# Where a norm takes its reciprocal root: ScalarE's table and VectorE's reciprocal, or Newton's steps on GpSimd

## The chip, the cores and the metric

The kernel runs on one core of a Trainium2 chip, in one launch. A core has five engines that work side by side, each through its own instructions in order: PE (TensorE, matrix products into PSUM), DVE (VectorE), ACT (ScalarE), POOL (GpSimd) and SP (SyncE, which here only issues transfers). The metric is the device time of one execution in microseconds (us), the median of several; lower is better.

## The reference, cut to what matters

A block of six sublayers over 2048 positions of 256 features, all in float32: feed-forward, attention, feed-forward, then the same three with other weights. Each sublayer is preceded by a layer norm, and the feed-forward of the first kind has an RMS norm in its middle. These norms are what the change is about.

```python
def _layernorm(x, axis=-1, eps=1e-05):
    m = jnp.mean(x, axis=axis, keepdims=True)
    v = jnp.var(x, axis=axis, keepdims=True)
    return (x - m) / jnp.sqrt(v + eps)

def rms_norm(x):                       # inside _L0_ffn_ref, over 1024 hidden values
    eps = jnp.finfo(x.dtype).eps.astype(jnp.float32)
    xf = x.astype(jnp.float32)
    inv = jax.lax.rsqrt(jnp.mean(xf * xf, axis=-1, keepdims=True) + eps)
    return (xf * inv).astype(x.dtype)
...
x = x + 0.5 * _L0_ffn_ref(_layernorm(x, axis=-1), L0_ffn_w_gate_up, L0_ffn_w_proj)
x = x + _L0_attn_ref(_layernorm(x, axis=-1), L0_attn_W_qkv, L0_attn_W_o)
x = x + 0.5 * _L0_ffn_ref(_layernorm(x, axis=-1), L0_ffn_w_gate_up, L0_ffn_w_proj)
x = x + 0.5 * _L1_ffn_ref(_layernorm(x, axis=-1), L1_ffn_w_gate, L1_ffn_w_up, L1_ffn_w_down)
x = x + _L1_attn_ref(_layernorm(x, axis=-1), ...)
x = x + 0.5 * _L1_ffn_ref(_layernorm(x, axis=-1), L1_ffn_w_gate, L1_ffn_w_up, L1_ffn_w_down)
```

`_L0_ffn_ref` makes its weights ternary (per group of 64), takes `silu(gate) * up`, the RMS norm, and a projection. `_L1_ffn_ref` takes `silu(gate) * up`, keeps the two largest of every four hidden values, and projects. Both attentions are causal with 16 heads of 16.

## The kernel before

**Tiling.** Features lie on the 128 partitions (two halves of 128, `DC = 2`), positions along the free dimension, cut into four chunks of 512 (`CH`, `NCH`). A chunk of x stays in SBUF from start to end (`xs[c]`), its normed form in `xns[c]`. The stages are called f0, attention 0, f1, f2, attention 1, f3. In the times below they run about from 0 to 212, 212 to 755, 755 to 877, 877 to 1085, 1085 to 1645 and 1645 to 1830 us.

**A step.** The order of the work on PE, DVE, ACT and POOL is written out by the program itself, through Python generators that hand over at `yield`. In a feed-forward stage a step is one of the eight blocks of 128 hidden values of a chunk: `gate_up0` (L297) or `gate_up` (L271) multiplies on PE, `member` (L310) takes Silu on ACT (L313) and multiplies by `up` on DVE (L314). In stages f0 and f1, `parts_of` (L326) splits each block into a rounded part (ACT, L328) and a rest (DVE, L335), squares it (ACT, L333) and adds the squares on POOL (L334). In f2 and f3, `sparsify` (L398) compares and selects on DVE (L408 to L436). After a chunk's blocks the next chunk's steps carry its projection along: `tail0` (L349) or `tail1` (L441). At the start f0 also makes the weights ternary (`quantize`, L130), six DVE instructions for each of 12 tiles. In an attention a step is one block of 128 keys of one group of four heads: scores, maxima on DVE (L721), exponentials on ACT (L792), and products with the values on PE (L807).

**Background.** The layer norms of the chunks to come wait in a queue, `background`. Each step calls `pull` (L194), which moves the first two of them on to their next `yield`. `ready(c)` (L200) pulls until chunk c's norm is through. At the end of an attention `gate` holds norms back before their root.

**A layer norm** (L234) goes: sum of the two halves on POOL (L242); two or three steps later the mean by a matmul with the matrix `mean_m`, whose entries are 1/256 (L246); x minus mean on DVE (L248); squares on ACT (L251); their sum on POOL (L253); two steps later a matmul again (L259) and `root`; one step later `spread`, and two multiplies on POOL that write `xn` (L264).

**The RMS norm** in `tail0`: the sums of squares go through a matmul with `ones_m` (L373), then `root`, a step in between, the second half of the projection, `spread`, and then `add` (L365): a product on DVE (L367) and the addition to x on POOL (L368).

**`root` and `spread`** (L205 to L222). The matmul leaves every position's value in all 128 rows. DVE's transpose by blocks of 32 (L209) turns it so that a tile of 128 x 16 holds each value once per block; the root is taken on that small tile. ACT takes the square root with scale and eps (L211), DVE the reciprocal (L216), and a second transpose (L218) spreads the result over 128 x 512 again. ACT works its functions from a table that must be loaded; Sqrt, Silu and Exp lie in different ones, so that the compiler puts an ACT_TABLE_LOAD ahead of a root and another ahead of the next Silu or Exp. Abs, Sign, Square, copies and Identity need none.

**Queues.** SP issues nearly all transfers, ACT the four loads of x. No transfer is issued by POOL.

Of the kernel before, what the change touches and what calls it, by code (L numbers as in the profile page):

```python
# [12 lines left out]
F32 = mybir.dt.float32  # L13
BF16 = mybir.dt.bfloat16
F32R = mybir.dt.float32r
AF = mybir.ActivationFunctionType
ALU = mybir.AluOpType
AX = mybir.AxisListType
# [2 lines left out]
P = 128  # L21
S = 2048
E = 256
# [3 lines left out]
SLOT = 32  # L27
G = 4
F = 1024
FC = F // P  # L30
CH = 512
# [16 lines left out]
def macaron_kernel(ctx: ExitStack, tc: tile.TileContext, a, out):  # L48
    nc = tc.nc

    cpool = ctx.enter_context(tc.tile_pool(name="const", bufs=1))
# [10 lines left out]
    def ps_one(name):  # L62
        return ps3.tile([P, CH], F32, tag="one", name=name)
# [43 lines left out]

    mean_m = cpool.tile([P, P], F32, name="mean_m")
    nc.vector.memset(mean_m, 1.0 / E)
    ones_m = cpool.tile([P, P], F32, name="ones_m")  # L110
    nc.vector.memset(ones_m, 1.0)
    eps_ln = cpool.tile([P, 1], F32, name="eps_ln")
    nc.vector.memset(eps_ln, 1e-5)
    eps_rms = cpool.tile([P, 1], F32, name="eps_rms")
    nc.vector.memset(eps_rms, 4 * float(np.finfo(np.float32).eps))


    lpool = ctx.enter_context(tc.tile_pool(name="ln", bufs=1))
# [4 lines left out]
    w0pool = ffn0_scope.enter_context(tc.tile_pool(name="weights0", bufs=1, side="right"))  # L123
    wgu0 = w0pool.tile([P, DC, 2 * F], F32R, name="wgu0")
    wp0 = w0pool.tile([P, FC, E], F32R, name="wp0")
    raw_scope = ExitStack()
# [3 lines left out]
    def quantize(i):  # L130
# [19 lines left out]
        aw = qp.tile([P, 512], BF16, tag="aw", bufs=4, name=f"aw{i}")  # L150
        nc.scalar.activation(aw, raw, AF.Abs)
        sg = qp.tile([P, 512], BF16, tag="sg", bufs=4, name=f"sg{i}")
        nc.scalar.activation(sg, raw, AF.Sign)
        yield
# [50 lines left out]
    def root(ps, eps, scale, name):  # L205


        tt = lpool.tile([P, CH // SLOT, SLOT], F32, tag="tt", name=f"tt_{name}")
        nc.vector.transpose(tt.rearrange("p b s -> p (b s)"), ps)  # L209
        r = lpool.tile([P, CH // SLOT], F32, tag="r", bufs=3, name=f"r_{name}")  # L210
        nc.scalar.activation(r, tt[:, :, 0], AF.Sqrt, bias=eps, scale=scale)  # L211
        return r

    def spread(r, pool, bufs, name):

        nc.vector.reciprocal(r, r)  # L216
        sd = pool.tile([P, CH], F32, tag="sd", bufs=bufs, name=f"sd_{name}")
        nc.vector.transpose(  # L218
            sd.rearrange("p (b s) -> p b s", s=SLOT),
            r.unsqueeze(2).to_broadcast([P, CH // SLOT, SLOT]),  # L220
        )
        return sd  # L222


    def split(c, hp, name):

        xn = xns[c]
        top = hp.tile([P, DC, CH], F32R, tag="xtop", bufs=2, name=f"xt_{name}")
        nc.vector.tensor_copy(top, xn)
        rest = hp.tile([P, DC, CH], F32R, tag="xrest", bufs=2, name=f"xr_{name}")  # L230
        nc.vector.tensor_tensor(rest, xn, top.bitcast(F32), ALU.subtract)  # L231
        return top, rest

    def layernorm(c, name, slack=0):  # L234

        pending[c] += 1
        asked.add(name)

        def pieces():
            x, xn = xs[c], xns[c]  # L240
            s = lpool.tile([P, CH], F32, tag="s", bufs=2, name=f"s_{name}")
            nc.gpsimd.tensor_tensor(s, x[:, 0, :], x[:, 1, :], ALU.add)  # L242
            for _ in range(2 + slack):
                yield
            pm = ps_one(f"pm_{name}")
            nc.tensor.matmul(pm, lhsT=mean_m, rhs=s, start=True, stop=True)  # L246
            xc = lpool.tile([P, DC, CH], F32, tag="xc", bufs=2, name=f"xc_{name}")
            nc.vector.tensor_tensor(  # L248
                xc, x, pm.unsqueeze(1).to_broadcast([P, DC, CH]), ALU.subtract
            )  # L250
            nc.scalar.activation(xn, xc, AF.Square)  # L251
            v = lpool.tile([P, CH], F32, tag="s", bufs=2, name=f"v_{name}")
            nc.gpsimd.tensor_tensor(v, xn[:, 0, :], xn[:, 1, :], ALU.add)  # L253
            yield
            yield
            while gate[0]:
                yield
            pv = ps_one(f"pv_{name}")
            nc.tensor.matmul(pv, lhsT=mean_m, rhs=v, start=True, stop=True)  # L259
            r = root(pv, eps_ln, 1.0, f"ln_{name}")  # L260
            yield
            sd = spread(r, lpool, 2, f"ln_{name}")
            for dc in range(DC):
                nc.gpsimd.tensor_tensor(xn[:, dc, :], xc[:, dc, :], sd, ALU.mult)  # L264
            pending[c] -= 1
            yield

        return pieces()


# [39 lines left out]
    def member(pg, hp, name, to=None):  # L310
        sl = hp.tile([P, CH], F32, tag="sl", bufs=3, name=f"sl_{name}")
        to = sl if to is None else to
        nc.scalar.activation(sl, pg[:, 0, :], AF.Silu)  # L313
        nc.vector.tensor_tensor(to, sl, pg[:, 1, :], ALU.mult)  # L314
        return to

    def steps0(c, xp, hp, own, name):
# [3 lines left out]
        tops = [  # L321
            hp.tile([P, 4, CH], F32R, tag="hr", bufs=3, name=f"ht_{name}_{q}") for q in range(2)
        ]
        rests = hp.tile([P, FC, CH], F32R, tag="h", bufs=2, name=f"hl_{name}")

        def parts_of(f, h):  # L326
            top = tops[f // 4][:, f % 4, :]
            nc.scalar.copy(top, h)  # L328
            if f == 0:
                nc.scalar.activation(ss, h, AF.Square)  # L330
            else:
# [17 lines left out]
    def tail0(c, ss, parts, hp, own, name):  # L349


        def project(dc):
            po = ps_one(f"po_{name}_{dc}")
            for f in range(FC):
                for part in range(2):
                    nc.tensor.matmul(  # L356
                        po,
                        lhsT=wp0[:, f, dc * P : (dc + 1) * P],
                        rhs=parts[f][part],
                        start=f == 0 and part == 0,  # L360
                        stop=f == FC - 1 and part == 1,
                    )
            return po

        def add(dc, po):  # L365
            y = hp.tile([P, CH], F32, tag="sl", bufs=3, name=f"y_{name}_{dc}")
            nc.vector.tensor_tensor(y, po, inv, ALU.mult)  # L367
            nc.gpsimd.tensor_tensor(xs[c][:, dc, :], y, xs[c][:, dc, :], ALU.add)  # L368

        po = project(0)  # L370
        yield
        pss = ps_one(f"pss_{name}")
        nc.tensor.matmul(pss, lhsT=ones_m, rhs=ss, start=True, stop=True)  # L373
        r = root(pss, eps_rms, 4.0 / F, f"rms_{name}")
        yield
        after = project(1)
        inv = spread(r, own, 1, f"rms_{name}")
        add(0, po)
        yield
        add(1, after)  # L380
        yield
# [75 lines left out]
    def feed_forwards(stages, beside, own=None):  # L457


        with tc.tile_pool(name=f"ffn_{stages[0][1]}", bufs=1) as hp:  # L460
# [4 lines left out]
            for s, (kind, stage, order) in enumerate(stages):  # L465
                for at, c in enumerate(order):
# [32 lines left out]
                    if kind == 0:  # L499
                        try:  # L500
                            next(work)
                        except StopIteration as end:
                            tail = ((0, 1, 2, 3), tail0(c, *end.value, hp, own, name), done)
                    else:
                        last = s == len(stages) - 1 and c == order[-1]
                        tail = ((4, 5), tail1(c, h, name, last), done)
# [594 lines left out]

    load_x(0, nc.scalar)
    ln = layernorm(0, "f0_0")
    for k in range(6):
        next(ln)
        if k in (0, 2, 4, 5):
            next(quants[0])
            next(quants[0])
# [119 lines left out]
```

## Time and profile before

| what | us |
|---|---|
| median of 3 runs (lowest, highest) | 1829.09 (1828.29, 1836.65) |
| the profiled execution | 1831.77 |
| its span, first to last instruction | 1830.0 |
| PE busy | 1648.4 |
| DVE busy | 1314.3 |
| ACT busy | 911.8 |
| POOL busy | 347.0 |
| ACT_TABLE_LOAD for roots (L211), 24 | 30.8 |
| ACT_TABLE_LOAD for Silu (L313), 19 | 24.4 |
| ACT_TABLE_LOAD for Exp (L792), 8 | 10.3 |
| the roots themselves (L211), 32 | 10.3 |
| the reciprocals (L216), 32 | 7.5 |

By stage, the busy time of each engine and the share of its clock that PE was granted (the view by windows; after the times stand the numbers of instructions in brackets):

| window, us | PE | DVE | ACT | POOL | PE clock |
|---|---|---|---|---|---|
| 0 to 26 | 6.5 | 20.2 | 12.8 | 7.8 | 1.00 |
| 26 to 90 | 36.0 | 55.5 | 24.2 | 23.3 | 0.81 |
| 90 to 212 | 106.9 | 72.8 | 65.7 | 69.3 | 0.93 |
| 212 to 755 | 509.2 | 406.7 | 310.9 | 47.8 | 0.99 |
| 755 to 877 | 100.6 | 83.4 | 69.8 | 70.4 | 0.93 |
| 877 to 1085 | 198.0 | 138.4 | 64.8 | 45.6 | 0.98 |
| 1085 to 1645 | 518.6 | 425.7 | 316.8 | 71.1 | 0.98 |
| 1645 to 1700 | 48.0 | 38.6 | 21.2 | 11.8 | 1.00 |
| 1700 to 1830 | 124.6 | 73.1 | 25.6 | 0.0 | 1.00 |

How to read the lines that follow. A line of the timeline has the start from the span's start, the duration, the engine (a q behind it is its sequencer, which only issues or waits), the line of the program, the operation, out<-in by the program's names, the shape written<-read and the count; in square brackets stands how long the engine had been idle before it, and what ended that. A line of a group has xcount, then busy time and mean ns of one, then the idle time before them and its causes. A line of waits has who waited, for whom, and then us in total, times and the longest. PE's durations are modelled and overlap: of matmuls in a row, the starts tell the pace.

### The profile page before, as it was taken

The numbers are of one execution on the slowest core, as the hardware profiler recorded it, in microseconds if no ns is written. First come the engines' busy times: TensorE is split into PE (matmuls) and PEld (weight loads), VectorE is DVE, ScalarE is ACT, GpSimd is POOL, SyncE is SP. The second block draws the span as 40 slices with busy tenths as digits, with TensorE's granted clock in tenths as the row PEclk, the third lists the DMA queues.
The fourth block names the chain that finished last, engine by engine and source line by source line (L and its number), as shares of the span: only waits on it lengthen the run. The fifth ranks groups of instructions, "written<-read, shape, count | busy, mean of one in ns | idle before, by whom it ended". The sixth has DMA issues, their size and how long they took to land.

```text
span 1830.0 us, 26213 instructions
## 1 busy us (share of the span) xinstructions
PE 1648.4 (90%) x10299; PEld 782.5 (43%) x10300; DVE 1314.3 (72%) x2368; ACT 911.8 (50%) x1220; POOL 347.0 (19%) x346
## 2 busy tenths in 40 slices
PE   4498888999999999788899998899999999988999
PEld 2365543444434443366444444334434434433443
DVE  7865687787788884466666677778788888816664
ACT  4365354555565667555423325445565556674221
POOL 3355520200000001265411232122001000012000
PEclk9799899999999999999999999999999999999999
DMA  4003332212211110200000334222122110000000
GB/s 138 2 1 105 114 95 79 72 54 76 93 41 47 30 30 1 78 1 1 13 0 1 103 109 130 66 85 90 48 65 90 46 46 28 11 2 0 12 12 23
DMA packets 50508, 93.06 MB, mean 51 GB/s; under 512 B 5424, under 2 KB 33072, under 8 KB 50128
## 3 DMA queue, kind: packets, MB, share of 16 engines
q1 hardware_dynamic: 49296, 89.28, 15.9%
q10 hardware_dynamic: 1088, 2.10, 0.4%
q8 instruction: 81, 1.33, 0.3%
q14 instruction: 43, 0.35, 0.1%
HBM read 59.51 MB, written 27.26 MB: 47 GB/s over the span
## 4 chain that ended last, share of the span: by engine, by line
PE 62%; DVE 19%; ACT 4%; issue 2%; POOL 2%; DMA 1%; SPq 0%; DVEq 0%; ACTq 0%; POOLq 0%
PE pav L807 14%; PE pst L772 12%; PE pq L710 11%; DVE mx L721 8%; PE pg_f L276 7%; PE po_f L287 5%; PE pg_f L301 2%; PE pwo L848 2%; PE pp_k L557 2%; PE pp_q L557 1%; PE po_f L356 1%; DVE ge_f L408 1%; PE pv L622 1%; PE pst L780 1%; PE pq L718 1%
## 5 line engine op out<-in xcount | busy, mean ns | idle before, releaser
L721 DVE TENSOR_REDUCE mx<-pq 128x1 f32<-128x512 f32 (+3 forms) x1280 | 696.7, 602 | 132.8 <-PE pq L718 65.4
L792 ACT ACTIVATE pT<-pst 128x1024 f32<-128x1024 f32 (+3 forms) x616 | 536.2, 897 | 335.8 <-PE pst L772 170.7
L710 PE MATMUL pq<-k,q 105*128 105x512 bf16 (+7 forms) x1280 | 385.9, 349 | 53.2 <-DVE mx L721 46.4
L772 PE MATMUL pst<-q,k 99*128 99x512 bf16 (+7 forms) x1280 | 356.5, 352 | 10.6 <-ACT pT L792 6.7
L807 PE MATMUL pav<-pT,va 128*32 128x256 f32 (+1 forms) x4608 | 324.7, 377 | 6.2 <-DVE yt L828 5.0
L276 PE MATMUL pg_f<-xn,wgu 128*128 128x512 f32 x512 | 230.5, 602 | 15.0 <-DVE hr_f L314 15.0
L772 PEld LDWEIGHTS <-k 105*128 105x128 bf16 (+1 forms) x1280 | 111.5, 98 | 233.7 <-issue 168.3
L833 POOL TENSOR_TENSOR zt<-yt,rd 128x64 f32<-128x64 f32 x128 | 42.1, 329 | 807.3 <-DVE rd L832 803.0
L807 PEld LDWEIGHTS pav<-pT,va 128*32 128x32 f32 x4608 | 106.3, 108 | 191.5 <-issue 136.8
L710 PEld LDWEIGHTS <-q 105*128 105x128 bf16 (+1 forms) x1280 | 122.9, 98 | 128.9 <-issue 26.5
L313 ACT ACTIVATE sl_f<-pg_f 128x512 f32<-128x512 f32 x128 | 75.9, 593 | 174.7 <-PE pg_f L276 98.3
L276 PEld LDWEIGHTS pg_f<-xn,wgu 128*128 128x128 f32 x512 | 97.4, 192 | 142.8 <-issue 115.1
L301 PE MATMUL pg_f<-xt_f,wgu 128*128 128x512 f32 x256 | 101.0, 478 | 37.8 <-DVE sl_f L314 20.9
L287 PE MATMUL po_f<-h_f,wd 128*128 128x512 f32 x256 | 112.6, 593 | 1.4 <-DVE h_f L436 1.4
L718 PE MATMUL pq<-mask_qk,ident_b 128*128 128x128 bf16 x512 | 105.4, 222 | 0.0
L780 PE MATMUL pst<-mask_kq,ident_b 128*128 128x128 bf16 x512 | 103.1, 221 | 0.0
L334 POOL TENSOR_TENSOR ss_f<-ss_f,sq_f 128x512 f32<-128x512 f32 x56 | 85.2, 1521 | 88.8 <-ACT sq_f L333 88.2
L314 DVE TENSOR_TENSOR hr_f<-sl_f,pg_f 128x512 f32<-128x512 f32 x64 | 43.7, 683 | 69.1 <-ACT sl_f L313 68.8
L828 DVE STREAM_TRANSPOSE yt<-pav 128x128 f32<-128x128 f32 x128 | 39.8, 311 | 71.1 <-PE pav L807 71.1
L301 PE MATMUL pg_f<-xr_f,wgu 128*128 128x512 f32 x256 | 86.0, 419 | 1.5 <-DVE xr_f L231 1.5
L314 DVE TENSOR_TENSOR sl_f<-sl_f,pg_f 128x512 f32<-128x512 f32 x64 | 43.7, 682 | 60.2 <-ACT sl_f L313 59.8
L301 PEld LDWEIGHTS pg_f<-xt_f,wgu 128*128 128x128 f32 x256 | 51.7, 208 | 80.8 <-DVE sl_f L314 27.5
(134 smaller groups left out, 1755.1 us busy)
## 6 DMA issues: line engine op xcount, KB each, us to landing
k<-dk SPq DMA_DIRECT2D x80, 384.0 KB
dk<-p_k SPq DMA_DIRECT2D x48, 256.0 KB
dq<-p_q SPq DMA_DIRECT2D x48, 256.0 KB
q<-dq SPq DMA_DIRECT2D x32, 384.0 KB
x<-in_xT ACTq DMA_DIRECT2D x4, 512.0 KB
raw<-in_w_gu SPq DMA_DIRECT2D x8, 256.0 KB
wgu<-in_w_gu SPq DMA_DIRECT2D x1, 2048.0 KB
cs_k<-in_cos_sin SPq DMA_DIRECT2D x4, 512.0 KB
```

Source lines behind the costliest of these rows:

```text
L276: nc.tensor.matmul(pg[:, half, :], lhsT=wgu[:, dc, half * F + f * P : half * F + (f + 1) * P], rhs=xn[:, dc, :], start=dc == 0, stop=dc == ...
L287: nc.tensor.matmul(po, lhsT=w[:, f, dc * P : (dc + 1) * P], rhs=h[:, f, :], start=f == 0, stop=f == FC - 1,)
L301: nc.tensor.matmul(pg[:, half, :], lhsT=wgu0[:, dc, half * F + f * P : half * F + (f + 1) * P], rhs=xp[part][:, dc, :], start=part == 0 an ...
L314: nc.vector.tensor_tensor(to, sl, pg[:, 1, :], ALU.mult)
L334: nc.gpsimd.tensor_tensor(ss, ss, sq, ALU.add)
L710: nc.tensor.matmul(pq, lhsT=qs[n][0:rows, hh, t * P : (t + 1) * P], rhs=ks[n, kc][0:rows, hh, 0:w], start=True, stop=kc < c,)
L718: nc.tensor.matmul(pq[:, w - P : w], lhsT=ident_b, rhs=mask_qk, start=False, stop=True)
L721: nc.vector.tensor_reduce(mxs[n][:, t, hh, kc : kc + 1], pq, AX.X, ALU.max)
L772: nc.tensor.matmul(ps[i][:, lo:CH], lhsT=ks[n, kc][0:rows, hh, t * P : (t + 1) * P], rhs=qs[n][0:rows, hh, lo:CH], start=True, stop=kc < c,)
L780: nc.tensor.matmul(ps[i][:, lo : lo + P], lhsT=ident_b, rhs=mask_kq, start=False, stop=True)
L792: nc.scalar.activation(pT[:, :, lo:CH], pair[:, :, lo:CH], AF.Exp, scale=0.25)
L807: nc.tensor.matmul(acc[hh * SLOT : (hh + 1) * SLOT, a:b], lhsT=va[kc][:, t, v0 : v0 + SLOT], rhs=pTs[hh // 2][:, hh % 2, a:b], start=kb == ...
```

## The change

The root is no longer taken from a table. `root` now makes four small tiles of 128 x 16. DVE computes v = scale * value + eps, and a first guess of 1/sqrt(v): v's bits, read as an integer, times -0.5 plus the constant 0x5F3759DF, written as the bits of r. POOL then computes m = -v/2 and three times r = r * (1.5 + m * r * r), in four instructions each: thirteen POOL instructions for a norm. `spread` loses its reciprocal. eps becomes a number in place of a tile, and the RMS norm's matmul uses `mean_m` with the factor 256 moved into the scale, so that `ones_m` and the tiles for eps go. A layer norm has one `yield` more between `root` and `spread`, and the first one, which the program draws by hand at the start, is drawn seven times in place of six. The RMS norm has no step more.

```diff
-    ones_m = cpool.tile([P, P], F32, name="ones_m")
-    nc.vector.memset(ones_m, 1.0)
-    eps_ln = cpool.tile([P, 1], F32, name="eps_ln")
-    nc.vector.memset(eps_ln, 1e-5)
-    eps_rms = cpool.tile([P, 1], F32, name="eps_rms")
-    nc.vector.memset(eps_rms, 4 * float(np.finfo(np.float32).eps))
+    eps_ln = 1e-5
+    eps_rms = 4 * float(np.finfo(np.float32).eps)
...
-        r = lpool.tile([P, CH // SLOT], F32, tag="r", bufs=3, name=f"r_{name}")
-        nc.scalar.activation(r, tt[:, :, 0], AF.Sqrt, bias=eps, scale=scale)
+        def small(what):
+            return lpool.tile([P, CH // SLOT], F32, tag=what, bufs=2, name=f"{what}_{name}")
+
+
+        v, m, w, r = small("nv"), small("nm"), small("nw"), small("r")
+        nc.vector.tensor_scalar(v, tt[:, :, 0], scale, eps, ALU.mult, ALU.add)
+        nc.vector.tensor_scalar(
+            r.bitcast(I32), v.bitcast(I32), -0.5, float(0x5F3759DF), ALU.mult, ALU.add
+        )
+        nc.gpsimd.tensor_scalar(m, v, -0.5, None, ALU.mult)
+        for _ in range(3):
+            nc.gpsimd.tensor_tensor(w, r, r, ALU.mult)
+            nc.gpsimd.tensor_tensor(w, w, m, ALU.mult)
+            nc.gpsimd.tensor_scalar(w, w, 1.5, None, ALU.add)
+            nc.gpsimd.tensor_tensor(r, r, w, ALU.mult)
         return r
 
     def spread(r, pool, bufs, name):
 
-        nc.vector.reciprocal(r, r)
...
             r = root(pv, eps_ln, 1.0, f"ln_{name}")
             yield
+            yield
             sd = spread(r, lpool, 2, f"ln_{name}")
...
-        nc.tensor.matmul(pss, lhsT=ones_m, rhs=ss, start=True, stop=True)
-        r = root(pss, eps_rms, 4.0 / F, f"rms_{name}")
+        nc.tensor.matmul(pss, lhsT=mean_m, rhs=ss, start=True, stop=True)
+        r = root(pss, eps_rms, 4.0 * E / F, f"rms_{name}")
...
-    for k in range(6):
+    for k in range(7):
         next(ln)
         if k in (0, 2, 4, 5):
```

There are 24 layer norms (six stages of four chunks) and 8 RMS norms (two stages of four).

More of the change, by code (lines that the diff above doesn't have):

```diff
@@ L15 @@
 F32R = mybir.dt.float32r
+I32 = mybir.dt.int32
 AF = mybir.ActivationFunctionType
```

## The prediction

> **What bounds the kernel now.** I read four views, coarse to fine. First the busy shares on the page and TensorE's own list of waits, to see which engine sets the pace and what it waits for:
>
> ```profile
> PE 1648.4 (90%) x10299; PEld 782.5 (43%) x10300; DVE 1314.3 (72%) x2368; ACT 911.8 (50%) x1220; POOL 347.0 (19%) x346
> ...
> PE pg_f L301 <- DVE sl_f L314: 20.9, 11, 4.1
> PE psq L156 <- DVE sc L159: 16.9, 6, 6.5
> PE pg_f L276 <- DVE hr_f L314: 15.0, 10, 4.0
> ```
>
> TensorE is 90% busy. A better norm can only win back idle time of PE, and only where the norm causes it. The candidates are the waits of the feed-forward matmuls for the gate product (L314), which stands behind Silu on ACT: 20.9 + 15.0 = 35.9 us. The 16.9 us at L156 belong to the quantization at the start, where DVE sets the pace.
>
> Second, the instructions of the line with the root, and one place in time:
>
> ```profile
> L211 ACT ACT_TABLE_LOAD  x24: 1283/1283/1283, 13.0 to 1685.2; - x24
> ...
> 104.39 1.28 ACT L211 ACT_TABLE_LOAD   x1
> ...
> 106.78 0.33 ACT L211 ACTIVATE r_ln_f<-tt_ln_f,eps_ln 128x16 f32<-128x16 f32 x1 [1.11 <-DVE tt_ln_f L209]
> 107.12 1.28 ACT L313 ACT_TABLE_LOAD   x1
> ...
> 108.42 0.60 ACT L313 ACTIVATE sl_f<-pg_f 128x512 f32<-128x512 f32 x1
> ...
> 109.05 0.69 DVE L314 TENSOR_TENSOR sl_f<-sl_f,pg_f 128x512 f32<-128x512 f32 x1 [1.72 <-ACT sl_f L313]
> ...
> 109.79 1.22 PE L301 MATMUL pg_f<-xt_f,wgu 128*128 128x512 f32 x2 [2.54 <-DVE sl_f L314]
> ```
>
> From 104.39 to 108.42 ACT does nothing but fetch a table, wait for the transpose, take the root and fetch Silu's table back; PE ends up idle for 2.54 us. That is the loss the edit can remove.
>
> Third, the same spot in the second use of the feed-forward (stage f1), where two norms fall into one step:
>
> ```profile
> 825.19 1.28 ACT L211 ACT_TABLE_LOAD   x1
> ...
> 830.94 1.35 POOL L334 TENSOR_TENSOR ss_f<-ss_f,sq_f 128x512 f32<-128x512 f32 x1 [9.42 <-ACT sq_f L333]
> ...
> 832.23 0.71 DVE L218 STREAM_TRANSPOSE sd_rms_f<-r_rms_f 128x512 f32<-128x512 f32 x1
> ...
> 844.06 1.22 PE L301 MATMUL pg_f<-xt_f,wgu 128*128 128x512 f32 x2 [4.07 <-DVE sl_f L314]
> ```
>
> Here the chain of waits runs ACT's loads, then POOL (832 to 837), then DVE (837 to 844), then PE. From 826 to 831 POOL is idle; from 831 on it is nearly full. New POOL work fits only into that hole.
>
> Fourth, what POOL does to DVE, from the quantization:
>
> ```profile
> 62.41 0.42 DVE L168 TENSOR_TENSOR q<-big,sg 128x512 bf16<-128x512 bf16 x1
> ...
> 67.11 5.59 POOL L264 TENSOR_TENSOR xn<-xc_f,sd_ln_f 128x512 f32<-128x512 f32 x4 [1.54 <-DVE sd_ln_f L218]
> ...
> 71.49 1.50 DVE L168 TENSOR_TENSOR q<-big,sg 128x512 bf16<-128x512 bf16 x1
> ```
>
> The same DVE instruction takes 0.42 us with POOL idle and 1.50 us beside a POOL multiply: a DVE instruction with two SBUF inputs waits out the POOL instruction in flight (L314 and L721, which read PSUM, keep their times).
>
> **The change, part by part.** *Removed from ACT.* The built program has 6 table loads in place of 52: 46 x 1.283 = 59.0 us, and 32 roots x 0.322 = 10.3 us, with 21.9 us of idle time before them. ACT is half idle, so little of it counts. What counts is PE's idle time behind it, by place:
> - 109.79 (2.54) and 114.91 (1.61). The second lies mostly behind the splits on DVE (xr 2.19 us beside POOL). After the gap matmul pairs take 1.05 us where they took 0.63, which comes back as well. I take 3.8.
> - Start of f1, where Silu's first load stays but the second pair goes: 765.57 (2.10), 768.53 (0.85). I take 2.5.
> - Start of f3: 1674.56 (3.37), 1691.17 (0.95), 1696.78 (1.91). The stretch is DVE-bound with SBUF inputs; 39 new POOL instructions fall into it. I take 3.0 of 6.2.
> - Attention: 239.69 (0.66), 253.55 (0.66), 1139.72 (0.93). I take 2.0.
>
> Together 11.3 us; all of them, with 837.87 (1.44) and 871.74 (1.46), would be 18.5 (with nothing added for the clock).
>
> In the Trainium skill, "ScalarE: Activation LUTs", section "What ACT_TABLE_LOAD costs", a switch costs 1283 ns and another 1380 ns of drain. The trace shows only the first part: the load at 107.12 ends at 108.40, and Silu starts at 108.42. By the page 46 switches would be 122 us rather than 59.0, and the gain would be larger by up to a factor of two.
>
> *DVE.* 32 reciprocals go (3.8 + 1.9 + 1.8 = 7.5 us) and 64 scale-and-add instructions of 128x16 come. Their nearest row is L733 (below), 0.187 us: 12.0; bounds 0.059 (memset of 128x1) and 0.236 (the reciprocal), 3.8 to 15.1. Net +4.5 us, some 0.14 on each norm. DVE also no longer waits for ACT's root before the next transpose (3.6 + 1.9 + 1.5 = 7.0 us).
>
> *POOL.* Thirteen dependent instructions of 128x16 for each of 32 norms. The trace has none; the nearest:
>
> ```profile
> L833 POOL TENSOR_TENSOR zt<-yt,rd 128x64 f32<-128x64 f32 x128 | 42.1, 329 | 807.3 <-DVE rd L832 803.0 <-DMA k<-dk 4.4
> ...
> L733 DVE TENSOR_TENSOR neg<-neg 128x16 f32<-128x16 f32 x64 | 12.0, 187 | 2.2
> ...
> 0.73 0.20 POOL masks.py:197 MEMSET ident<- 128x128 f32 x1 [0.29 <-POOLq L1218]
> ...
> 1.01 0.29 POOL masks.py:199 TENSOR_SCALAR_AFFINE_SELECT ident<-ident 128x128 f32<-128x128 f32 x1
> ```
>
> L833 takes 0.29 undisturbed, the 128x512 multiplies 1.27: 0.98 for 448 elements, so 128x16 is about 0.185. The affine select, which needs the memset, starts 0.08 after its end. So 13 x 0.265 = 3.4 us a norm. From below: 13 x (0.10 + 0.08) = 2.3, by the memsets of 128x1. From above: each waits behind one DVE instruction of 0.41 and holds the next up in turn, 13 x 0.65 = 8.5. I take 3.4, and 8.5 only where DVE is full of SBUF instructions.
>
> The Trainium skill speaks against this use: "GPSIMD Engine Reference", section 4.1, sends elementwise arithmetic to VectorE and calls GPSIMD about twice as slow with two inputs. At this size the rows don't show it (0.185 against 0.187). By the rule a norm would take 13 x 2 x 0.187 = 4.9 us, and the losses below grow by about 1.5 us at each place on the path.
>
> Where the 3.4 us show:
> - Start. Before, xn starts at 20.39 and the cast L229 at 24.92. Now DVE's guess is ready at about 16.6, POOL's steps run against the quantization (8.5), so the transpose falls at 25, xn ends at 28.4: +3.5. By the low price the step moved past one tile alone costs 1; a fuller collision 5.
> - Chunks 1 and 2 of f0 (58 to 70, DVE-bound): 26 x 0.185 = 4.8 on DVE, less the 1.52 it waited for the root at 60.14: +3.3. Bounds 0 and 8.
> - Four steps with a layer norm and an RMS norm together (128, 166, 825, 859): two chains in one queue, 826.4 + 6.8 = 833.2 against 832.23, and behind them the sums (L334) and residual adds (L368) move back, which Silu's buffers wait for: +1.5 each, 6.0. Bounds -1 and +5 each.
> - The last RMS norm of f0 (204.93): the second y waits for PE until 210.31 anyway; the chain to it comes out at 211.6: +1.3. Bounds 0 and 4.
>
> Together 14.1. The other norms have two steps to spare: in attention POOL is under 20% busy, and behind the new instructions stand only the small multiplies L833, whose result is wanted two steps later.
>
> *Moved.* The extra step puts a layer norm's transpose and its two multiplies one step later; at the end of f0 one matmul group each of k and q for chunk 1 moves past a gate-up step (1.9 us), and two k loads on SP move past one and four others. Nothing waits for these loads by more than the 3.8 us that PE spends on q<-qx. I put this at 0; without cover, 2.
>
> *Sum.* The profiled execution took 1831.77 us (span 1830.0 and 1.8 around it), 2.7 over the median of 1829.09. 1831.77 - 11.3 + 14.1 = 1834.6; in terms of the median **1832 us**. About 0.5% (9.1 us) is what a measurement of this kernel can tell from no change, so my forecast is no change: chance 0.42, own range 1820 to 1838.
>
> **Rivals.**
> - *The chains stay hidden* (faster). For it: POOL 19% busy, the 9.42 us hole, a step more. Against it: the hole closes at 831. All 18.5 gained, the low price, and 3.5 lost at the start and the moves: 1829.1 - 15 = 1814. Chance 0.25.
> - *The shared way into SBUF* (slower). One mechanism: small POOL instructions alternate with DVE's SBUF ones, so a norm takes 8.5 us instead of 3.4, in the feed-forward stages; DVE, in order, then stands at the transpose. From a price of about 5 us a norm it decides. Start +5, f0 +8, four double steps +5 each, RMS +4: 37, less 17 gained, since half of the stalls at f3 and f1 only change owner where DVE waits: 1829.1 + 20 = 1849. For it: 0.42 against 1.50 above. Against it: DVE waiting at the transpose lets POOL run free. Chance 0.33.
> - That the loads stay is no rival: the built program has 6.
>
> **The range** is 1815 to 1850; it leaves out part of both rivals. Faster 0.25, within 0.5% 0.42, slower 0.33, from these cases.
>
> **What would show it.** ACT busy near 842 us with 6 loads; no gap at 109.79 and 765.57; POOL near 347 + 32 x 13 x 0.185 = 424 us. A norm's thirteen instructions from first to last: 3.4 in attention, more in f0. PE's first L301 near 29 instead of 25.66. sd_rms of the f1 steps about 1 us later and the 4.07 us gap still there. I am wrong if that gap closes (then the ACT loads, not POOL, fed it), or if a norm takes over 5 us where DVE reads PSUM.

## The result, and the profile after

The changed kernel takes 1863.28 us (median of 4 runs, 1862.00 to 1863.99) beside 1828.69 us for the kernel before on the same chip: ratio 1.0168, 95% interval 1.0142 to 1.0195. It is slower by about 31 to 35 us, outside the predicted range. In this section and the next, a ratio is to the kernel before, and "+20 us" means that ratio less one, times 1829.

The page and the groups of instructions by line of the changed kernel: busy time of each engine, then the table loads that are left (count, mean ns).

```profile
PE 1662.3 (89%) x10299; PEld 789.5 (42%) x10300; DVE 1313.9 (71%) x2397; ACT 843.8 (45%) x1142; POOL 461.6 (25%) x762
...
L323 ACT ACT_TABLE_LOAD x3 | 3.8, 1283 | 21.0 <-PE pg_f L311 11.4 <-PE pg_f L286 9.3 <-issue 0.4
L802 ACT ACT_TABLE_LOAD x2 | 2.6, 1283 | 0.0
L148 ACT ACT_TABLE_LOAD x1 | 1.3, 1283 | 1.2 <-PEq L1228 1.2
```

ACT does what was expected of it: 911.8 us become 843.8, and six loads are left (the one at L148 stands ahead of the program's first Abs). But PE is busy 13.9 us longer with the same 10299 instructions. Its waits and those of DVE, in us in all, times, and the longest:

```profile
PE pg_f L311 <- DVE sl_f L324: 25.6, 9, 4.2
PE pg_f L311 <- DVE xt_f L238: 20.2, 3, 10.1
PE pg_f L286 <- DVE hr_f L324: 15.9, 7, 5.7
PE psq L153 <- DVE sc L156: 10.5, 5, 3.6
PE pp_k L567 <- POOL xn L274: 10.3, 4, 4.9
```

```profile
DVE sd_rms_f L227 <- POOL r_rms_f L221: 30.3, 8, 5.5
...
DVE sd_ln_f L227 <- POOL r_ln_f L221: 6.0, 4, 3.1
```

Four things are new or larger. The gate product's wait (L311 for L324) is up from 20.9 to 25.6 us. The wait for the split of x at the start of a feed-forward (`xt_f`) is up from 9.7 to 20.2 us, while that of the quantization (L153) is down from 16.9 to 10.5. The matmuls of k now wait 10.3 us for `xn` from POOL; the kernel before had no such line. And DVE stands 36.3 us at the transposes (L227), waiting for POOL's roots. The place where this starts, in the timeline of the changed kernel (start, duration, engine, line, and in brackets the idle time before and what ended it):

```profile
129.62 0.26 POOL L216 TENSOR_SCALAR nm_ln_after_f<-nv_ln_after_f 128x16 f32<-128x16 f32 x1 [3.58 <-DVE nv_ln_after_f L212]
...
133.71 0.22 POOL L221 TENSOR_TENSOR r_ln_after_f<-r_ln_after_f,nw_ln_after_f 128x16 f32<-128x16 f32 x1
...
133.90 0.26 POOL L216 TENSOR_SCALAR nm_rms_f<-nv_rms_f 128x16 f32<-128x16 f32 x1
...
137.54 0.22 POOL L221 TENSOR_TENSOR r_rms_f<-r_rms_f,nw_rms_f 128x16 f32<-128x16 f32 x1
...
137.79 0.71 DVE L227 STREAM_TRANSPOSE sd_rms_f<-r_rms_f 128x512 f32<-128x512 f32 x1 [5.51 <-POOL r_rms_f L221]
...
139.15 0.68 DVE L324 TENSOR_TENSOR sl_f<-sl_f,pg_f 128x512 f32<-128x512 f32 x1
...
139.88 0.50 PE L311 MATMUL pg_f<-xt_f,wgu 128*128 128x512 f32 x1 [2.12 <-DVE sl_f L324]
```

A layer norm's chain and an RMS norm's chain run one after the other on POOL, 129.62 to 137.76. DVE stands at the RMS transpose for 5.51 us, and the gate product behind it in DVE's order comes at 139.15, so PE stands for 2.12 us. What PE does after the stop is in the table by stretches. A row has the stretch, its length, the busy time of PE, PEld, DVE, ACT and POOL with the numbers of instructions, and then the share of the clock that TensorE was granted:

```profile
132.00:136.00 4.00, 4.00 (x19) 3.22 (x18) 0.28 (x1) 0.03 (x1) 3.10 (x14) 1.00 0.00 0
136.00:140.00 4.00, 1.88 (x9) 1.21 (x8) 2.17 (x4) 1.61 (x3) 3.26 (x8) 1.00 0.00 0
140.00:144.00 4.00, 3.77 (x9) 2.43 (x10) 4.00 (x6) 1.63 (x3) 4.00 (x4) 0.57 0.00 0
```

In the four microseconds after the stop the clock is 0.57, and 9 matmuls keep PE busy for 3.77 us, where 19 took 4.00 at 132 to 136. So a stop is paid for once while PE stands and again while it is slow. By line, the longer PE time is mostly in the feed-forward matmuls of L311 (7.1 us more for the same count) and in those of k and q (L567, 5.2 us more).

### The profile page after: what moved, and what is told of

Same layout as the page of the kernel before. It is cut to its first block, busy times and chain, and to the rows that moved or that the text cites. A ratio compares the mean times of both kernels' runs of the same rounds, so it can differ in the third digit from the quotient of the medians.

```text
span 1862.0 us, 26541 instructions
## 1 busy us (share of the span) xinstructions
PE 1662.3 (89%) x10299; PEld 789.5 (42%) x10300; DVE 1313.9 (71%) x2397; ACT 843.8 (45%) x1142; POOL 461.6 (25%) x762
## 4 chain that ended last, share of the span: by engine, by line
PE 61%; DVE 19%; POOL 5%; issue 3%; ACT 2%; DMA 1%; SPq 0%; DVEq 0%; ACTq 0%; POOLq 0%
PE pav L817 14%; PE pst L782 12%; PE pq L720 10%; DVE mx L731 8%; PE pg_f L286 7%; PE po_f L297 6%; PE pg_f L311 2%; PE pp_k L567 2%; PE pwo L858 2%; PE pp_q L567 2%; PE pv L632 1%; PE pq L728 1%; PE pst L790 1%; DVE ge_f L418 1%; DVE h_f L446 1%
## 5 line engine op out<-in xcount | busy, mean ns | idle before, releaser
L286 PE MATMUL pg_f<-xn,wgu 128*128 128x512 f32 x512 | 231.6, 605 | 16.1 <-DVE hr_f L324 15.9
L311 PE MATMUL pg_f<-xt_f,wgu 128*128 128x512 f32 x256 | 103.8, 490 | 53.1 <-DVE sl_f L324 25.6
L324 DVE TENSOR_TENSOR hr_f<-sl_f,pg_f 128x512 f32<-128x512 f32 x64 | 43.7, 683 | 74.4 <-ACT sl_f L323 74.4
L311 PEld LDWEIGHTS pg_f<-xt_f,wgu 128*128 128x128 f32 x256 | 53.9, 215 | 89.3 <-DVE sl_f L324 29.6
L311 PE MATMUL pg_f<-xr_f,wgu 128*128 128x512 f32 x256 | 90.3, 437 | 1.5 <-DVE xr_f L240 1.5
L324 DVE TENSOR_TENSOR sl_f<-sl_f,pg_f 128x512 f32<-128x512 f32 x64 | 43.5, 680 | 50.8 <-ACT sl_f L323 50.6
```

Source lines behind the costliest of these rows:

```text
L286: nc.tensor.matmul(pg[:, half, :], lhsT=wgu[:, dc, half * F + f * P : half * F + (f + 1) * P], rhs=xn[:, dc, :], start=dc == 0, stop=dc == ...
L311: nc.tensor.matmul(pg[:, half, :], lhsT=wgu0[:, dc, half * F + f * P : half * F + (f + 1) * P], rhs=xp[part][:, dc, :], start=part == 0 an ...
```

## The experiments

Theory A: GpSimd's dependent chain is late at the transposes, and VectorE stands there in order. Theory B: the extra step brings `xn` too late. Theory C, made after the first four runs: GpSimd work costs by its amount, wherever it lies. All runs, with the median and the ratio to the kernel before:

| run | median us | ratio (95%) |
|---|---|---|
| e1 chains, no step | 1883.25 | 1.0273 (1.0250 to 1.0295) |
| e2 step alone | 1852.56 | 1.0108 (1.0091 to 1.0125) |
| e3 chains on VectorE | 1907.01 | 1.0400 (1.0379 to 1.0420) |
| e4 guess alone, with step | 1838.74 | 1.0035 (1.0024 to 1.0047) |
| e5 guess alone, no step | 1813.94 | 0.9896 (0.9876 to 0.9917) |
| e6 chains of layer norms only | 1843.73 | 1.0052 (1.0036 to 1.0068) |
| e7 chains of RMS norms only | 1845.40 | 1.0062 (1.0047 to 1.0077) |
| e8 layer norm's chain a step later | 1883.35 | 1.0272 (1.0257 to 1.0288) |
| e9 k half a step later | 1866.64 | 1.0187 (1.0164 to 1.0210) |
| e10 RMS chain first | 1868.63 | 1.0198 (1.0175 to 1.0220) |
| e11 8 instructions, no step | 1841.86 | 1.0061 (1.0038 to 1.0083) |
| e12 8 instructions, step, RMS first, k later | 1849.70 | 1.0103 (1.0072 to 1.0135) |
| e13 step alone, k past a group | 1842.01 | 1.0041 (1.0025 to 1.0057) |
| e14 as e13, no step at the start | 1842.63 | 1.0049 (1.0031 to 1.0068) |
| e15 6 instructions, no step | 1822.39 | 0.9958 (0.9935 to 0.9982) |
| e16 4 instructions, no step | 1812.69 | 0.9891 (0.9867 to 0.9916) |
| e17 3 on VectorE, no step | 1827.65 | 0.9974 (0.9961 to 0.9987) |

**e1 and e2: the step and the chains apart.**

```diff
# e1, against the change
             yield
-            yield
...
-    for k in range(7):
+    for k in range(6):
# e2, against the kernel before
             yield
+            yield
...
-    for k in range(6):
+    for k in range(7):
```

> The change without its extra step: one yield between root and transpose, as in the kernel before; Newton's steps stay on GpSimd. Theory A (GpSimd's dependent chain is late at the transposes, and VectorE stands there in order): the layer norms' transposes now come a step earlier and wait too, so nothing is won: 1858 to 1875 us, and the waits of sd_ln on GpSimd grow from 6.0 us. Theory B (the extra step brings xn too late for the matmuls of k and the splits): 1840 to 1850 us, and TensorE's waits pp_k for xn (10.3 us) and pg_f for xt_f (20.2 us) fall back to about 0 and 10.

> The kernel before with the extra step alone: ScalarE's root and VectorE's reciprocal stay. Theory A: 1826 to 1832 us. Theory B: 1840 to 1850 us, with the waits pp_k for xn near 10 us and pg_f for xt_f near 20 us, as in the change.

Both theories were half right, though e1 came out above A's range and e2 2.6 us above B's. The step alone costs +20 us (B), with the waits of the k matmuls for `xn` (11.6 us) and of L302 for `xt_f` (18.5, before 9.7) that B asked for. But without the step the change gets worse by another 19 us (A): the transposes of the layer norms now come before the chain is through, and DVE stands at them 39.6 us and at the RMS ones 24.2.

**e3 and e4: the chains elsewhere, and not at all.**

```diff
# e3: the thirteen instructions
-        nc.gpsimd.tensor_scalar(m, v, -0.5, None, ALU.mult)
+        nc.vector.tensor_scalar(m, v, -0.5, None, ALU.mult)
...
# e4: they are left out
-        nc.gpsimd.tensor_scalar(m, v, -0.5, None, ALU.mult)
-        for _ in range(3):
...
```

> The change with the same thirteen instructions of each norm on VectorE in place of GpSimd. At VectorE's 0.175 us and starts 0.21 us apart a norm takes 13 x 0.21 = 2.7 us of VectorE in place of 3.9 to 7 on GpSimd, and two norms of one step no longer queue behind ss and x. Theory A: the 30.3 us of VectorE's waits at sd_rms go, but 32 x 2.7 = 87 us of VectorE come, of which only those in the feed-forward stages (some 22 norms, 60 us, most of it in VectorE's idle time) can show: 1830 to 1850 us. Theory B: 1855 to 1870 us, pp_k and xt_f waiting as in the change.

> The change with no Newton step: the guess of VectorE is used as the root, which leaves out the refinement; all else, the extra step too, stays. Theory A: what is left is the change without GpSimd's share: 1829 less most of the 11.3 us of ScalarE's loads, 1812 to 1825 us. Theory B: 1835 to 1850 us, with the waits pp_k for xn still near 10 us.

e3 went far above both ranges: no wait for POOL is left at the transposes, DVE is busy 74 us longer than in e4 (1390.0 against 1316.0), and the run is 67 us longer than e4. So work on DVE at these places is paid for nearly in full, and a chain needs no queue on GpSimd to be dear. e4 fell in B's range, with the wait at pp_k still 11.4 us. The chains cost 1.0168 less 1.0035, 24 us of the loss. The rest of e4 is the step less the gain.

**e5: the gain by itself.** (e4 with one `yield` and `range(6)`.)

> The guess alone (no Newton step, which leaves out the refinement) and without the extra step: the change's gain by itself. If the parts add up, e4 less what the step alone cost (e2: 1852.6 against about 1829 to 1832, so 20 to 24 us): 1838.7 - 22 = 1817 us, bounds 1812 to 1822. If the step costs only beside ScalarE's slow root (the two share the same idle time of TensorE), it stays at 1830 to 1838.

-19 us, as the sum of parts said. So without ScalarE's loads, and without any chain or step, 19 us are to be won, and the step costs 25 us beside the guess (e4 against e5) and 20 beside the root (e2).

**e6, e7, e8, e10: which chain, and in which order.**

```diff
# e6 (e7: "rms"); e8 and e10 move the calls
+        if not name.startswith("ln"):
+            return r
         nc.gpsimd.tensor_scalar(m, v, -0.5, None, ALU.mult)
```

> The change with Newton's steps for the 24 layer norms alone; the 8 RMS norms use the guess (their refinement is left out). Theory A (VectorE stands at the RMS transpose, the only one with no step to spare, behind two chains): the RMS transpose needs nothing of GpSimd any more, so about the time of e4: 1839 to 1845 us. Theory C (any GpSimd instruction in the feed-forward costs, as a share of the 32 norms): 3/4 of the 24.5 us between e4 and the change: 1855 to 1859 us.

> The change with Newton's steps for the 8 RMS norms alone; the 24 layer norms use the guess. Theory A: the waits at sd_rms fall from 30.3 us to some 12 (the 4 double steps lose the first chain of about 4 us each, the 4 single ones keep theirs), most of the cost stays where only one chain stood: 1846 to 1856 us. Theory C: 1/4 of the 24.5 us: 1843 to 1847 us, with e6 the dearer of the two by 12 us. If A and C are both off, e6 and e7 don't add up to the change.

The layer norms' chains alone add 3 us to e4, the RMS norms' alone 5; both together 24. C, which asked 18 for the layer norms, is out by e6 (the 5 of e7 would suit it), and e7 is just under the range of A. A plain sum is out too: two thirds of the price, 16 us with some 7 either way by the intervals, come only where the two kinds meet.

```diff
# e8: a layer norm's chain one step after its guess
-            r = root(pv, eps_ln, 1.0, f"ln_{name}")
+            r, refine = root(pv, eps_ln, 1.0, f"ln_{name}")
             yield
+            refine()
             yield
# e10: in the step loop, its chain after the RMS norm's
+                        holding[0] = True
                         pull()
                         if tail and f in tail[0]:
                             next(tail[1])
+                        holding[0] = False
+                        while late:
+                            late.popleft()()
```

> The whole change, but a layer norm's thirteen GpSimd instructions are issued one step after its guess, so that an RMS norm of the same step comes first in GpSimd's queue. Theory A: each of the 4 double steps gives back the layer norm's chain ahead of the RMS one, about 3.9 us of VectorE's 5.5 us wait: 1844 to 1856 us. Theory C: the same work in the same places, 1860 to 1867 us; if the layer norms' own transposes now wait (sd_ln above 20 us in sum), slower than the change.

> The whole change, each instruction kept in its step, but where an RMS norm and a layer norm fall into one step the RMS norm's thirteen GpSimd instructions come first. If the 13 us by which the two kinds of chain together cost more than each alone (24.5 against 5.0 + 6.7 us) are the RMS transpose behind two chains, the waits at sd_rms fall from 30.3 us towards the 16.1 us of e7, and the time to 1849 to 1856 us. If they are something else (VectorE slowed by GpSimd), 1860 to 1866 us.

e8 missed both ranges, and its last clause came true: the layer norms now miss their own transposes (26.2 us at sd_ln), and it is slower than the change by 19 us. e10 missed both too. The wait at sd_rms fell as asked, from 30.3 to 16.0 us, and nothing came of it: the wait of the k matmuls for `xn` rose from 10.3 to 15.0 us, ACT's for x (Silu's buffers) from 15.5 to 22.7, and DVE's at sd_ln from 6.0 to 10.3. Its timeline at the same double step:

```profile
138.01 0.71 DVE L235 STREAM_TRANSPOSE sd_ln_after_f<-r_ln_after_f 128x512 f32<-128x512 f32 x1 [1.35 <-POOL r_ln_after_f L224]
...
141.61 2.93 POOL L282 TENSOR_TENSOR xn<-xc_after_f,sd_ln_after_f 128x512 f32<-128x512 f32 x2
...
142.93 2.07 PE L580 MATMUL pp_k<-xn,wqkv 128*128 128x512 f32 x2 [4.52 <-POOL xn L282]
```

Where PE had stood 2.12 us for the gate product and 0.71 for `xn`, it now stands 4.52 us for `xn`: the layer norm of a double step is wanted as soon as the RMS norm. Neither order of the two helped; what would take the 16 us away isn't shown.

**e9, e13, e14: what the step does.**

```diff
# e13 (e9: one yield at the second place alone, in the change)
                 nc.gpsimd.memset(va[0], 1.0)
                 yield
+                for _ in range(2 if layer else 0):
+                    yield
...
                 while f"after_{before}_1" not in asked or len(pools) == 1 and pending[1]:
                     yield
+                yield
+                yield
# e14 besides: the extra step of layernorm
+            if not name.startswith("f0_"):
                 yield
```

> The change, with the k and q matmuls of chunk 1 issued one step later in both layers, so that a gate-up group of TensorE lies between the issue of xn and the k matmuls that read it. If the extra step's price is TensorE standing in order at pp_k for an xn that is now issued right ahead of it (4.4 us at 182 and 5.2 us at 1008 with the step alone, 10.3 us in sum in the change), these waits go and the time falls by 8 to 14 us, to 1849 to 1855; the wait at the start and the split's near 82 us stay. If the step costs by something else, 1860 to 1866 us.

> The kernel before with the extra step, and the first k and q matmuls of each layer issued past one more gate-up group of TensorE (e9 moved them by half a step only, and its k matmuls stayed right behind xn: the waits at 188 and 1022 us were still 4.75 and 4.87). If the waits pp_k for xn (11.6 us with the step alone) are most of the step's price: they fall to 0 to 2 us, and the time from 1852.6 to 1840 to 1845 us. If the wait only moves to whoever stands behind them, 1848 to 1855 us.

> As e13, but the four layer norms of the start (stage f0) go without the extra step, so it stays only for those behind the feed-forwards. If the start's part is what the splits' waits show (xt_f 18.5 us in place of 9.7, less 4.9 that the quantization waits less): 2 to 5 us under e13. What then is left over the kernel before is neither the start nor pp_k.

e9 says nothing on the theory: two of its yields make a step there, so k's first matmuls stayed behind the same `xn` (their wait at 188 us is 4.75). e13 does what e9 was meant to do. First the kernel before, then the step alone (e2), at the k matmuls of chunk 1:

```profile
174.52 0.71 DVE L218 STREAM_TRANSPOSE sd_ln_after_f<-r_ln_after_f 128x512 f32<-128x512 f32 x1
...
175.42 2.48 POOL L264 TENSOR_TENSOR xn<-xc_after_f,sd_ln_after_f 128x512 f32<-128x512 f32 x2
...
177.29 1.95 PE L557 MATMUL pp_k<-xn,wqkv 128*128 128x512 f32 x4 [0.78 <-ACT va L633]
```

```profile
178.70 0.69 DVE L315 TENSOR_TENSOR sl_f<-sl_f,pg_f 128x512 f32<-128x512 f32 x1 [3.12 <-ACT sl_f L314]
180.18 0.71 DVE L218 STREAM_TRANSPOSE sd_ln_after_f<-r_ln_after_f 128x512 f32<-128x512 f32 x1
...
181.07 2.48 POOL L265 TENSOR_TENSOR xn<-xc_after_f,sd_ln_after_f 128x512 f32<-128x512 f32 x2
...
182.38 2.08 PE L558 MATMUL pp_k<-xn,wqkv 128*128 128x512 f32 x2 [4.40 <-POOL xn L265]
```

Before, the k matmuls follow `xn` while PE still has the values' matmuls (1.89 us) to do. With the step, the transpose stands behind the next block's gate product on DVE (178.70), and the k matmuls, issued in the same step as `xn`, are PE's next instruction: it stands 4.4 us. With one gate-up group between (e13) the waits for `xn` are 3.8 us (0 to 2 expected) in place of 11.6, here e2's line and then e13's, and of the step's +20 us +7.5 are left.

```profile
PE pp_k L558 <- POOL xn L265: 11.6, 5, 5.2
```

```profile
PE pp_k L558 <- POOL xn L265: 3.8, 3, 2.5
```

The start is not in it: e14 equals e13 within the intervals, where 2 to 5 us less were expected. What the last 7.5 us are wasn't settled: e13's profile is of its shortest run (1833.66 us, median 1842.01), and shows no loss to look at.

**e11, e15, e16, e17, and e12: shorter chains.** The root is still taken from the guess, with VectorE's first instruction making -v/2.

```diff
# e11: two plain steps, without the instruction for m
-        nc.gpsimd.tensor_scalar(m, v, -0.5, None, ALU.mult)
-        for _ in range(3):
+        for _ in range(2):
# e15: one step of third order
+        nc.gpsimd.tensor_tensor(w, r, r, ALU.mult)
+        nc.gpsimd.tensor_tensor(y, w, m, ALU.mult)
+        nc.gpsimd.tensor_scalar(w, y, 1.50387391, 2.50606084, ALU.mult, ALU.add)
+        nc.gpsimd.tensor_tensor(w, w, y, ALU.mult)
+        nc.gpsimd.tensor_scalar(w, w, 1.87706155, None, ALU.add)
+        nc.gpsimd.tensor_tensor(r, r, w, ALU.mult)
# e16: one Newton step with fitted constants
+        nc.gpsimd.tensor_tensor(w, r, r, ALU.mult)
+        nc.gpsimd.tensor_tensor(w, w, m, ALU.mult)
+        nc.gpsimd.tensor_scalar(w, w, 1.04954966, 1.52518106, ALU.mult, ALU.add)
+        nc.gpsimd.tensor_tensor(r, r, w, ALU.mult)
# e17: the same on VectorE
+        nc.vector.tensor_tensor(w, r, r, ALU.mult)
+        nc.vector.scalar_tensor_tensor(w, w, 1.04954966, m, ALU.mult, ALU.mult)
+        nc.vector.scalar_tensor_tensor(r, w, 1.52518106, r, ALU.add, ALU.mult)
```

> Eight GpSimd instructions in place of thirteen (two Newton steps of three; -v/2 comes from VectorE's own scale-and-add), no extra step. Without the step thirteen cost 69 us over the guess alone (e1 against e5), 5.3 us each; if the cost is in proportion, 1814 + 42 = 1856 us; if it counts only from where the chain reaches the next step's transpose (some 2 us), much less: 1820 to 1840 us, which could beat the kernel before.

> No extra step; per norm six GpSimd instructions: one step of third order with fitted constants (relative error of the root at most 2.5e-5, in place of three Newton steps). By the line through e5 (0 instructions, 1813.9), e11 (8, 1841.9) and e1 (13, 1883.3), which bends upwards: 1824 to 1836 us. If a norm costs only from some 5 instructions on, 1820 us or less; if it costs by the crossing to GpSimd and back alone, 1835 us or more.

> No extra step; per norm four GpSimd instructions: one Newton step with fitted constants, which leaves the root with a relative error of up to 8e-4. In proportion to e11: 1814 + 14 = 1828 us; if four lie in the idle time between two steps, 1814 to 1820 us; if the crossing alone costs, 1830 us or more.

> No extra step; the one fitted Newton step of e16 (root within 8e-4), but on VectorE, which does it in three instructions with its two-operation form. If VectorE's occupied time is what costs, as its standing did in e1, e11 and e15 (about 1.1 us of run time for each us that it stands at the transposes), then 32 x 3 x 0.21 = 20 us of VectorE at the 0.78 of e3 (68 us for 87) add 16 us: 1826 to 1832 us, and four on GpSimd (1812.7) are the better place. If what counts is the crossing between the engines, no slower than e16: 1808 to 1815 us.

e11 came between its proportional 1856 us and the threshold's range, e15 and e16 a little under theirs. Together they make a curve: 0, 4, 6, 8 and 13 instructions give -19, -20, -8, +11 and +50 us. Four are free, 13 cost 69. The waits of DVE for POOL explain it; those of e16 and then of e1:

```profile
DVE sd_rms_f L225 <- POOL r_rms_f L219: 2.2, 2, 1.2
DVE sd_ln_f L225 <- POOL r_ln_f L219: 0.4, 1, 0.4
```

```profile
DVE sd_ln_f L227 <- POOL r_ln_f L221: 29.6, 13, 3.1
DVE sd_rms_f L227 <- POOL r_rms_f L221: 24.2, 8, 3.8
DVE sd_ln_after_f L227 <- POOL r_ln_after_f L221: 10.0, 6, 2.3
```

In sum 2.6 us (e16), 10.5 (e15), 23.9 (e11) and 63.8 (e1): from e16 to e1, 61.2 us more of standing make the run 70 us longer, 1.14 us for each. That price is one of the kernels without the step. Beside e4, e7 pays 5 us for 16.1 us of standing (0.3 each), the change 24 for 36.3 (0.7) and e10 30 for 26.3 (1.1). e17 came inside its first range: three instructions on VectorE make DVE busy 22 us longer than in e5 (1338.3 against 1316.2) and the run 14 us longer, where four on GpSimd cost nothing. So in the kernels without the step VectorE's time, standing or working, is what a norm is mostly paid in; with the step it is not all, since e10 stands 10 us less than the change and is no faster.

The Trainium skill, "GPSIMD Engine Reference", section 4.1, would have sent these products to VectorE, with GpSimd about twice as slow. Measured at 128x16, an undisturbed product takes 0.22 us on GpSimd and 0.175 on VectorE (1.25 times), and the slower engine is the better place, because the other one is wanted.

> The eight-instruction chain with the extra step, RMS first, and k and q of chunk 1 a step later. If the parts add up: 1863 less 10 (k), less 10 (order), less 3 to 5 (five instructions fewer in each RMS chain): 1836 to 1842 us, so about the kernel before; if the parts overlap, 1845 to 1850 us.

e12 came inside its second range: the parts overlap. Its k matmuls, moved as in e9, still wait 11.6 us for `xn`.

e16 (0.9891), e15 (0.9958) and, barely, e17 (0.9974) beat both kernels; e16's root is within 8e-4, e15's within 2.5e-5.

## Why the prediction was wrong

The sum had -11 us for ACT's loads, +14 for the chains and 0 for the step. The runs show -19 (e5), +24 (the change against e4) and +25 (e4 against e5), which add up to the measured +31 but for rounding, as each is the difference between two neighbours.

- **ACT's loads.** Right in the count (6), in ACT's busy time (842 forecast, 843.8), and that PE's idle time behind them is what can be won. Of the "all of them 18.5" I took 11.3, because the stretches looked bound by DVE; e5 shows 19 us. Mis-sized by 8 us. In e5's trace the waits for the gate product are 24.0 us in place of 35.9, which is near the 11.3, and PE is busy 5.9 us less with the same matmuls, for which the sum added little.
- **"Moved. I put this at 0; without cover, 2".** This is the step that failed. The extra step costs 20 us beside the root (e2), 25 beside the guess. I looked for who waits for the transfers and for a matmul group that moves past a gate-up, and not for who reads `xn` next on PE: the k matmuls, issued in the same step, which PE cannot pass. The cover had been the values' matmuls and DVE's free moment before the next gate product; e13 puts a cover back, and 12 of the 20 us with it. Where the other 8 lie stays open.
- **"Four double steps, +1.5 each".** Right in kind: two chains in one queue. In size, the transpose comes 8.2 us after the first POOL instruction (137.79 less 129.62), where I had 6.8; I priced the lateness against POOL's sums and residual additions only, and not DVE's standing (5.51 us) with the gate product behind it. The 24 us for all chains (change against e4) stand against 14.1 in my sum, and e6 and e7 put 16 of them where both kinds meet.
- **The price of a norm.** I took 13 x 0.265 = 3.4 us. Undisturbed it is 3.85: 0.215 to 0.258 us an instruction, starts 0.30 apart. Beside busy DVE work in the feed-forwards chains of 4.3 to 7.0 us occur, never 8.5. POOL's busy time is 461.6 us where I had 424.
- **The start.** +3.5 forecast; PE's first L311 comes at 27.90 instead of 25.66: +2.2. The chain's collision with the quantization, which I priced, doesn't explain it: without chain and step it comes at 27.62 (e5), and at 27.53 in e14, whose start is written as in the kernel before.
- **The clock.** I added nothing for it. PE is busy 13.9 us longer in a span that is 32.0 us longer; the mean granted clock is 0.961 in place of 0.974.
- **The rivals.** "The shared way into SBUF" had the sign, 1849 us, and that DVE stands at the transpose. Its mechanism, 8.5 us a norm, did not occur: the chain at 133.90 ran at its undisturbed 3.86 us while DVE stood, and beside busy DVE the longest took 7.0. "The chains stay hidden" is true of four instructions without the step (e16, at 1812.69 beside that rival's 1814), not of thirteen.
- **My signs.** Counted by the blocks of 128 hidden values, the gaps at 109.79 and 765.57 went, as said; two blocks behind the second a new one of 4.18 us stands (784.80), after two layer norms' transposes at which DVE waits for POOL. The gap of 114.91, which I had put down mostly to the splits on DVE and which still stands behind them, grew from 1.61 to 2.83 us (111.78). The 4.07 us gap stayed in part: behind the same block it is 3.22 us (865.84), and 4.08 us (830.73) stand a chunk earlier, where the kernel before had 3.87 (811.40). sd_rms of that f1 step was to come about 1 us later. It came 6.81 us after the gate product of its block in place of 2.37, 4.4 us later.

## What to carry to other kernels

Price a chain on a helper engine by what the engine that waits for it has queued behind the wait: here each microsecond that VectorE stood cost 1.14 us in the kernels without the step and 0.3 to 1.1 in three with it, while chains that ended about when their reader came (e16) cost nothing. Moving a producer one step later is not free because a step seems to be spare; find its next reader on every in-order engine, and what lies between the two in that engine's order. Shorten a chain (four instructions for thirteen) before moving or reordering it.

## What the hardware showed that was not expected

Undisturbed, a dependent GpSimd instruction of 128x16 takes 0.215 to 0.258 us, and its successor starts about 0.30 us after it, so a chain lasts longer than its busy time: 4 x 0.256 + 9 x 0.218 = 3.0 us of work in 3.85. After PE's stop of 2.12 us before 139.88 the granted clock was 0.57 over the next four microseconds, and pairs of the same matmuls took 1.05 us in place of 0.63. After the stop of 2.83 us before 111.78 the first pairs took 0.72 and 0.62 us, but from 113 to 118 the clock was 0.50. The Trainium skill, "TensorE: Matmul & The Clock Gate", section "HAM oscillation — how this bites in real kernels", warns of gaps over about 3.4 us; here both of these shorter ones were followed by a stretch at about half the clock. With e1 against e5, 27 of the 67 us that the span grew are longer PE time at the same work.
